# Scores of a pair of batches as one block of TensorE work, from a bank pool shared with the products, and the value products twelve places later

## Chip, cores, metric

The kernel runs on 1 core of one Trainium2 chip, in fp32. The metric is device time in microseconds (us). The result compares 4 runs of each kernel, made together; all are in the fast state. Times of one kernel agree within 0.2%, except where a range is given.

## The reference, cut to what matters

A batch is a graph of 128 nodes with 512 features; there are 128 batches, and every batch goes through four layers by itself. The fourth layer is attention with 8 heads, and the change is about its order.

```python
# x: (128, 128, 512); adj: (128, 128); all fp32
x = _layernorm(x + (adj @ x) @ w0 + bias0)            # layer 0
x = _layernorm(x + _L1_gnn_ref(x, W, a, beta, adj))   # layer 1: graph attention, one product with W
x = _layernorm(x + _L2_gnn_ref(x, adj, adj, b))       # layer 2: one product with adj, a maximum
# layer 3
q, k, v = (x @ w_qkv).reshape(b, n, 3, H, hd).transpose(2, 0, 3, 1, 4)   # H = 8, hd = 64
attn = softmax(where(adj == 0, -inf, q @ k.T * hd**-0.5))
o = (attn @ v) @ w_proj + b_proj
x = _layernorm(x + o + layernorm(o) * gamma + beta3)
```

## The kernel before

The kernel is written as chains, one or more per batch. A planner at build time asks every chain for its next step, takes the one that can start first (and of those the one with the lowest rank), and so fixes the order of instructions of each engine. On the chip the engines keep that order and wait for each other by semaphores. A step on TensorE names the buffers it needs; `tr`, `mm` and `sc` are PSUM tiles (`tr` and `mm` one bank each, `sc` two banks).

```python
BUFS = {
    "tr": 3, "mm": 3, "sc": 1,
    # ... buffers in SBUF: 16 batches (x) at once, 2 of xT, 6 of v, 2 of prT
}
TAIL = 8

def tiled(gr, before, bs=range(G)):          # G = 2: a pair of batches
    yield gr.qk
    if before:
        for b in range(G):
            yield before.rows[b]             # the pair before has its transposed probabilities
    got = yield use(
        "PE", 1.1 if len(bs) == 1 else 1.0,
        lambda: ("sc",) + ("pr",) * len(bs) + ("tr", "oT") * (G if before else 0),
        late=0.0, urgent=True,
    )
    gr.pr.extend(got[1 : 1 + len(bs)])
    score(gr, bs[0], got[0])                 # scores of the first batch
    if before:
        yield use("PE", 0.88 * G + 0.15, late=0.0, follow=True)
        attends(before, range(G), got[1 + len(bs) :])   # both attends of the pair before
    for b in bs[1:]:
        got = yield use("PE", 1.15, "sc", follow=True)  # waits for the one score buffer
        score(gr, b, got)                    # scores of the second batch

def score(gr, b, bs):
    sc = bank([P, 2, K, P], "sc")
    nodes = slice(b * P, (b + 1) * P)
    for c in range(K):
        for j in range(2):                   # 64 rows of the array: heads j = 0 and 1 beside each other
            rws = slice(j * HD, (j + 1) * HD)
            nc.tensor.matmul(sc[:, j, c, :], gr.qkT[rws, c, nodes], gr.qkT[rws, K + c, nodes],
                             start=True, stop=True)
    # ...

def attends(gr, bs, slots):
    for n, b in enumerate(bs):
        # ...
        p = bank([P, K, P], "tr")
        for c in range(K):
            for j in range(2):               # 64 columns of the array
                nc.tensor.matmul(p[j * HD : (j + 1) * HD, c, :],
                                 valued.v[:, (2 * c + j) * HD : (2 * c + j + 1) * HD],
                                 prT[:, j * K + c], start=True, stop=True)
        # ...

# in batch(i), after layer 2:
    plan.start(values(i, gr, valued), i + G)           # the product x @ w_v, with rank i + 2
    yield gr.scored[b]
    # ...
    nc.vector.tensor_tensor(pr, sc..., maskb..., op=ALU.add)   # one mask add of 128x1024
    give(bs)
```

Of the kernel before, what the change touches and what calls it, by code (L numbers as in the profile page):

```python
# [10 lines left out]
ALU = mybir.AluOpType  # L11
# [4 lines left out]
P = 128  # L16
D = 512
K = D // P
G = 2
H = 8  # L20
HD = D // H
# [5 lines left out]


BUFS = {
    "tr": 3, "mm": 3, "sc": 1,  # L30
    "x": 16, "yT": 4, "z": 2, "e": 2, "et": 1, "eT": 2, "ex": 2, "xT": 2, "v": 6, "qkT": 3,
    "pr": 2, "pt": 1, "xt": 2, "prT": 2, "oT": 2, "o": 2,
}
TAIL = 8
MARGIN = 1.0
LAND, ROW_LAND = 2.0, 0.0053

# [6 lines left out]
class Plan:  # L44
# [14 lines left out]
    def use(self, engine, work, take=None, late=0.05, urgent=False, follow=False):  # L59





        names = take if callable(take) else lambda: (take,) if take else ()
        return engine, work, names, late, 0 if follow else 1 if urgent else 2
# [4 lines left out]
    def done(self, event, late=0.0):  # L71
        event.left -= 1
        event.at = max(event.at, self.now + late)
        if not event.left:
            for r in event.chains:
                r["ready"] = max(r["ready"], event.at)
                self.step(r, None)

    def give(self, slot):
        name, i = slot  # L80
        self.slots[name][i] = self.now
# [13 lines left out]
    def at(self, r):  # L95
        engine, _, take, _, order = r["want"]
        early = min(MARGIN, r["ready"] / 20) if engine == "PE" and order else 0.0
        t = max(r["ready"] + early, self.free.get(engine, 0.0))
# [26 lines left out]
def gnn_stack_kernel(  # L125
# [17 lines left out]
    nc = tc.nc  # L143
# [9 lines left out]
    plan = Plan()  # L153
    use, give, done = plan.use, plan.give, plan.done

    def buf(shape, name):
        return work.tile(shape, F32, name=name, bufs=BUFS[name])

    def bank(shape, name):
        return ps.tile(shape, F32, name=name, bufs=BUFS[name])  # L160
# [40 lines left out]
    def product(lhs, rhs):  # L201

        p = bank([P, D], "mm")
        for k in range(K):
            nc.tensor.matmul(p, lhs(k), rhs(k), start=(k == 0), stop=(k == K - 1))  # L205
        return p
# [31 lines left out]
    maskb = const.tile([P, P], F32, name="maskb")  # L238
# [127 lines left out]
    class Group:  # L366


        def __init__(self):
            self.s = small.tile([P, G, 2], F32, name="s")  # L370
            self.logits = [Event(2) for _ in range(G // 2)]
            self.attention = [Event() for _ in range(G // 2)]
            self.turned, self.qk = Event(G), Event(K)
            self.rows, self.attended = ([Event() for _ in range(G)] for _ in range(2))
            self.scored = [Event() for _ in range(G)]
            self.heads, self.o, self.prT, self.sc, self.pr = {}, {}, [], {}, []
            self.eT, self.xT, self.qkT, self.slot, self.left = {}, None, None, {}, {}

        def read(self, name, of):
# [7 lines left out]
    def group(g):  # L387
        if g not in groups:
            groups[g] = Group()
            for h in range(G // 2):  # L390
                plan.start(attention1(groups[g], h), g * G + 2 * h - (8 if g * G >= NB - 8 else 0))
            for n in range(K):
                plan.start(query_key(groups[g], n // 2 * 2 + K * (n % 2)), g * G + n / K - (8 if g * G >= NB - 8 else 0))


            rank = g * G - (8 if g * G >= NB - 8 else 0)
            if g * G < NB - TAIL:
                plan.start(tiled(groups[g], groups.get(g - 1)), rank)
            else:
                for b in range(G):  # L400
                    plan.start(tiled(groups[g], None, (b,)), rank)
            if g * G >= NB - TAIL - G:
                for bs in ((0, 1),) if g * G < NB - G else ((0,), (1,)):
                    plan.start(attend(groups[g], bs), rank)
        return groups[g]
# [96 lines left out]
    def tiled(gr, before, bs=range(G)):  # L502
        yield gr.qk
        if before:
            for b in range(G):
                yield before.rows[b]
        got = yield use(
            "PE", 1.1 if len(bs) == 1 else 1.0,
            lambda: ("sc",) + ("pr",) * len(bs) + ("tr", "oT") * (G if before else 0),
            late=0.0, urgent=True,  # L510
        )
        gr.pr.extend(got[1 : 1 + len(bs)])
        score(gr, bs[0], got[0])
        if before:
            yield use("PE", 0.88 * G + 0.15, late=0.0, follow=True)
            attends(before, range(G), got[1 + len(bs) :])
        for b in bs[1:]:
            got = yield use("PE", 1.15, "sc", follow=True)
            score(gr, b, got)

    def score(gr, b, bs):

        sc = bank([P, 2, K, P], "sc")
        nodes = slice(b * P, (b + 1) * P)
        for c in range(K):
            for j in range(2):
                rws = slice(j * HD, (j + 1) * HD)
                nc.tensor.matmul(  # L528
                    sc[:, j, c, :], gr.qkT[rws, c, nodes], gr.qkT[rws, K + c, nodes],
                    start=True, stop=True,  # L530
                )
        gr.read("qkT", G)
        gr.sc[b] = sc, bs
        done(gr.scored[b], 0.15)

    def attend(gr, bs):
        for b in bs:
# [6 lines left out]
    def attends(gr, bs, slots):  # L544
        for n, b in enumerate(bs):
            valued, prT, bt = gr.heads.pop(b)

            p = bank([P, K, P], "tr")
            for c in range(K):
                for j in range(2):  # L550
                    nc.tensor.matmul(  # L551
                        p[j * HD : (j + 1) * HD, c, :],
                        valued.v[:, (2 * c + j) * HD : (2 * c + j + 1) * HD],
                        prT[:, j * K + c], start=True, stop=True,
                    )
            give(bt)
            give(valued.slot)
            gr.o[b] = p, slots[2 * n], slots[2 * n + 1]
        for b in bs:
            done(gr.attended[b], 0.2)  # L560

    def values(i, gr, event):
        b = i % G
        yield gr.turned
        bp = yield use("PE", 3.46, "mm", late=0.2)
        p = product(
            lambda k: gr.xT[:, k, b * P : (b + 1) * P], lambda k: wqkv_sb[:, k, 2 * D :]
        )
        bv = yield use("ACT", 0.6, "v", urgent=True)
        event.v = buf([P, D], "v")  # L570
        nc.scalar.copy(event.v, p)  # L571
        give(bp)
        gr.read("xT", G + K)
        event.slot = bv
        done(event)
# [19 lines left out]
    def batch(i):  # L595
        g, b = divmod(i, G)
        h = b // 2
        yield loaded[i]
        gr, xb = group(g), xs[i]
# [8 lines left out]
        p = product(lambda k: yT[:, k, :], lambda k: w0_sb[:, k, :])  # L608
# [8 lines left out]
        for j in range(2):  # L617
# [12 lines left out]
        p = product(lambda k: yT[:, k, :], lambda k: w1_sb[:, k, :])  # L630
# [15 lines left out]
        p = bank([P, D], "mm")  # L646
# [17 lines left out]
        biased = Event()  # L664
        plan.start(pool_add(xb, beta3_sb, biased), i)
        valued = Event()
        plan.start(values(i, gr, valued), i + G)

        yield gr.scored[b]
        sc, bs = gr.sc.pop(b)  # L670
        yield use("DVE", 1.22, urgent=True)
        pr, bpr = buf([P, H, P], "pr"), gr.pr.pop()
        nc.vector.tensor_tensor(  # L673
            pr, sc.rearrange("p j c m -> p (j c) m"),
            maskb[:, None, :].to_broadcast([P, H, P]), op=ALU.add,
        )
        give(bs)
        yield use("DVE", 1.22)
        nmx = small.tile([P, H], F32, name="nmx3")
        nc.vector.tensor_reduce(nmx, pr, axis=AX.X, op=ALU.max, negate=True)  # L680
# [21 lines left out]
        got = yield use("SP", 0.5, lambda: () if gr.prT else ("prT",) * G, late=4.0)  # L702
# [10 lines left out]
        p, ba, bo = gr.o.pop(b)  # L713
        yield use("ACT", 0.6, urgent=True)
        oT = buf([P, K, P], "oT")
# [4 lines left out]
        p = product(lambda k: oT[:, k, :], lambda k: wproj_sb[:, k, :])  # L720
# [22 lines left out]
    with tc.manual_schedule(  # L743
        engines={ENG.PE, ENG.DVE, ENG.Activation, ENG.Pool, ENG.SP}
    ):
        plan.start(loads(), 0)
        plan.start(adjacency(), 0)
        for i in range(NB):

            plan.start(batch(i), i if i < NB - 8 else i - 8)  # L750
        plan.run()
# [27 lines left out]
```

## Time and profile before

| | us |
|---|---|
| median time | 3294.3 (3293.8 to 3295.8) |
| span of the profiled run | 3291.2 |
| TensorE busy | 3269.0 |
| VectorE busy | 2663.6 |
| waits of TensorE that the profile lists | 9.7 |

The prediction below shows the lines on TensorE. How to read them: busy time of TensorE is no measure here, since the ends of matmuls are modelled; the distance from one start to the next is what a piece of work took. Two lines that come up again later are those of VectorE's mask add and of the division of probabilities by their sums (by-form groups of the kernel before; columns: line, engine, operation, tiles, shapes, count, then busy us and mean ns, then idle us before them and what ended it).

```profile
L691 DVE TENSOR_TENSOR pr<-pr,rs 128x1024 f32<-128x1024 f32 x128 | 192.0, 1500 | 4.4
L673 DVE TENSOR_TENSOR pr<-sc,maskb 128x1024 f32<-128x1024 f32 x128 | 156.2, 1220 | 57.3 <-PE sc L528 56.7
```

### The profile page before, as it was taken

The page shows a single profiled execution, that of the slowest core. Times are in us where ns is not written, and L with a number is a line of the kernel's source. Part 1 is how long each engine was busy: PE and PEld are TensorE (multiplying, and loading weights), DVE is VectorE, ACT ScalarE, POOL GpSimd, SP SyncE. Part 2 cuts the span into 40 slices and gives each one's busy share as a digit, 9 for nine tenths or more (in the row PEclk, how much of TensorE's full clock was granted, in tenths as well). Part 3 has the DMA queues.
Part 4 walks back from the last instruction along what each step waited for, and adds up shares of the span by engine and source line. Part 5 has one row for each costly group of instructions (what it writes and reads, how often), then busy time and mean ns, then how long its engine had stood idle before and what let it go on. Part 6 is the DMA issues. An engine that isn't in the chain of part 4 may idle for free.

```text
span 3291.2 us, 43479 instructions
## 1 busy us (share of the span) xinstructions
PE 3269.0 (99%) x14613; PEld 2064.7 (63%) x14613; DVE 2663.6 (81%) x5527; ACT 1186.9 (36%) x3457; POOL 965.6 (29%) x1031
## 2 busy tenths in 40 slices
PE   9999999999999999999999999999999999999998
PEld 5666666667565666566665656666566666656665
DVE  7879786996879868878788787869878787988867
ACT  3433433343433423333333333433333343334332
POOL 3223131331323314223233242313313131332322
PEclk9999999999999999999999999999999999999999
DMA  4323333223332333223233232332323323232232
GB/s 164 85 89 85 93 109 95 69 86 101 97 98 68 88 100 101 95 79 105 86 88 97 79 103 81 97 91 76 106 82 98 98 73 99 81 98 84 85 90 103
DMA packets 469760, 304.47 MB, mean 93 GB/s; under 512 B 319264, under 2 KB 401312, under 8 KB 469536
## 3 DMA queue, kind: packets, MB, share of 16 engines
q1 hardware_dynamic: 469536, 301.69, 30.8%
q8 instruction: 116, 1.90, 0.2%
q14 instruction: 108, 0.88, 0.1%
HBM read 158.93 MB, written 142.67 MB: 92 GB/s over the span
## 4 chain that ended last, share of the span: by engine, by line
PE 95%; DVE 3%; DMA 1%; SPq 1%; issue 0%; ACT 0%; POOL 0%; POOLq 0%; DVEq 0%; ACTq 0%
PE mm L205 51%; PE mm L485 27%; PE tr L213 6%; PE sc L528 4%; PE tr L551 3%; PE mm L647 3%; DVE st L171 0%; SPq L589 0%; DMA z<-s_d 0%; DVE x L640 0%; DVE x L192 0%; DVE x L612 0%; DMA s_d<-s 0%; DVE mv L173 0%; DVE pr L691 0%
## 5 line engine op out<-in xcount | busy, mean ns | idle before, releaser
L485 PE MATMUL mm<-xT,wqkv_sb 128*128 128x256 f32 x4096 | 908.4, 380 | 0.0
L205 PE MATMUL mm<-w_sb,yT 128*128 128x512 f32 x2048 | 904.6, 593 | 1.0 <-ACT yT L216 0.7
L178 POOL TENSOR_TENSOR rstd<-ve,neghalf 128x1 f32<-128x1 f32 x640 | 444.1, 694 | 1521.8 <-DVE ve L175 1267.0
L485 PEld LDWEIGHTS mm<-xT,wqkv_sb 128*128 128x128 f32 x4096 | 775.1, 190 | 146.8 <-issue 38.1
L205 PEld LDWEIGHTS mm<-w_sb,yT 128*128 128x128 f32 x2048 | 382.6, 190 | 452.5 <-issue 441.9
L205 PE MATMUL mm<-wproj_sb,oT 128*128 128x512 f32 x1024 | 453.6, 595 | 2.1 <-ACT oT L716 2.1
L205 PE MATMUL mm<-wqkv_sb,xT 128*128 128x512 f32 x1024 | 455.6, 593 | 0.0
L684 ACT ACTIVATE pr<-pr,nmx 128x128 f32<-128x128 f32 x1024 | 396.5, 389 | 109.1 <-DVE nmx L680 108.7
L171 DVE BATCH_NORM_STATS2 st<-x 128x6 f32<-128x512 f32 x512 | 349.4, 682 | 8.0 <-ACT x L655 5.4
L205 PEld LDWEIGHTS mm<-wproj_sb,oT 128*128 128x128 f32 x1024 | 192.1, 190 | 230.8 <-issue 220.5
L205 PEld LDWEIGHTS mm<-wqkv_sb,xT 128*128 128x128 f32 x1024 | 193.0, 190 | 216.4 <-issue 209.5
L198 POOL TENSOR_TENSOR x<-x,o 128x512 f32<-128x512 f32 x128 | 174.4, 1363 | 507.9 <-DVE o L724 507.5
L187 ACT ACTIVATE x<-x,nmr,rstd 128x512 f32<-128x512 f32 x256 | 205.1, 810 | 299.9 <-DVE nmr L185 286.3
L198 POOL TENSOR_TENSOR x<-x,beta_sb 128x512 f32<-128x512 f32 x128 | 174.4, 1365 | 208.0 <-DVE xt L661 185.6
L571 ACT COPY v<-mm 128x512 f32<-128x512 f32 x128 | 74.9, 586 | 427.1 <-PE mm L205 426.9
L216 ACT COPY yT<-tr 128x512 f32<-128x512 f32 x256 | 149.7, 585 | 210.5 <-PE tr L213 210.1
L619 DVE SCALAR_TENSOR_TENSOR scr<-x,wa_rows 128x512 f32<-128x512 f32 x256 | 200.2, 782 | 21.5 <-ACT x L187 16.4
L493 ACT ACTIVATE qkT<-mm 128x512 f32<-128x512 f32 x128 | 76.2, 595 | 363.4 <-PE mm L485 363.0
L198 POOL TENSOR_TENSOR x<-x,bias_sb 128x512 f32<-128x512 f32 x128 | 178.2, 1404 | 83.7 <-PE tr L213 74.3
L673 DVE TENSOR_TENSOR pr<-sc,maskb 128x1024 f32<-128x1024 f32 x128 | 156.2, 1220 | 57.3 <-PE sc L528 56.7
L691 DVE TENSOR_TENSOR pr<-pr,rs 128x1024 f32<-128x1024 f32 x128 | 192.0, 1500 | 4.4
L684 ACT ACTIVATION_READ_ACCUMULATOR pr<-pr,nmx 128x1 f32 x1024 | 192.4, 188 | 0.0
(64 smaller groups left out, 3501.2 us busy)
## 6 DMA issues: line engine op xcount, KB each, us to landing
p_d<-pt SPq DMA_DIRECT2D x128, 512.0 KB
prT<-p_d SPq DMA_DIRECT2D x128, 512.0 KB
x<-in_x SPq DMA_DIRECT2D x128, 256.0 KB
x_d<-xt SPq DMA_DIRECT2D x128, 256.0 KB
xT<-x_d SPq DMA_DIRECT2D x512, 64.0 KB
out<-x SPq DMA_DIRECT2D x128, 256.0 KB
z<-s_d SPq DMA_DIRECT2D x64, 128.0 KB
e_d<-et SPq DMA_DIRECT2D x64, 128.0 KB
```

What stands on the lines that cost most here:

```text
L171: nc.vector.bn_stats(st, src)
L178: nc.gpsimd.tensor_tensor(rstd, ve, neghalf, op=ALU.pow)
L187: nc.scalar.activation(xb, xb, AF.Identity, bias=nmr, scale=rstd)
L198: nc.gpsimd.tensor_tensor(dst, dst, other, op=ALU.add)
L205: nc.tensor.matmul(p, lhs(k), rhs(k), start=(k == 0), stop=(k == K - 1))
L213: nc.tensor.matmul(p[:, k, :], xb[:, k * P : (k + 1) * P], nodes, start=True, stop=True)
L216: nc.scalar.copy(yT, p)
L485: nc.tensor.matmul(p[:, j, :], wqkv_sb[:, k, (c + j) * P : (c + j + 1) * P], gr.xT[:, k, :], start=(k == 0), stop=(k == K - 1),)
L619: nc.vector.scalar_tensor_tensor(scr, xb, 1.0, wa_rows[:, j, :], op0=ALU.mult, op1=ALU.mult, accum_out=gr.s[:, b, j : j + 1],)
L673: nc.vector.tensor_tensor(pr, sc.rearrange("p j c m -> p (j c) m"), maskb[:, None, :].to_broadcast([P, H, P]), op=ALU.add,)
L684: nc.scalar.activation(pr[:, j, :], pr[:, j, :], AF.Exp, bias=nmx[:, j : j + 1], accum_out=sums[:, j : j + 1],)
L691: nc.vector.tensor_tensor(pr, pr, rs[:, :, None].to_broadcast([P, H, P]), op=ALU.mult)
```

## The change

The intent: put the scores of both batches of a pair side by side, followed by both attends of the preceding pair, so that TensorE enters its half-array modes once and leaves them once per pair. Two scores at once need four banks, so the score buffer is given up and products and scores share five banks. The mask add becomes two, one for each bank. The value products get rank i + 12 in place of i + 2; "twelve places later" and "late values" below mean this, counted from the batch's own rank.

```diff
-    "tr": 3, "mm": 3, "sc": 1,
+    "tr": 3, "mm": 5,
 TAIL = 8
+LATER = 12
@@ tiled
+        n = len(bs)
         got = yield use(
-            "PE", 1.1 if len(bs) == 1 else 1.0,
-            lambda: ("sc",) + ("pr",) * len(bs) + ("tr", "oT") * (G if before else 0),
+            "PE", 0.25 + 0.88 * n + (0.88 * G + 0.15 if before else 0),
+            lambda: ("mm", "mm", "pr") * n + ("tr", "oT") * (G if before else 0),
             late=0.0, urgent=True,
         )
-        gr.pr.extend(got[1 : 1 + len(bs)])
-        score(gr, bs[0], got[0])
+        for b in bs:
+            ps_b = [bank([P, K, P], "mm") for _ in range(2)]
+            # ... the same 8 matmuls, to ps_b[j][:, c, :]
         if before:
-            yield use("PE", 0.88 * G + 0.15, late=0.0, follow=True)
-            attends(before, range(G), got[1 + len(bs) :])
-        for b in bs[1:]:
-            got = yield use("PE", 1.15, "sc", follow=True)
-            score(gr, b, got)
+            attends(before, range(G), got)
+        # ... done(gr.scored[b]) for each
@@ batch
-        plan.start(values(i, gr, valued), i + G)
+        plan.start(values(i, gr, valued), i + LATER)
-        nc.vector.tensor_tensor(pr, sc..., maskb... [P, H, P], op=ALU.add)
-        give(bs)
+        for j in range(2):
+            # ... pr[:, j * K : (j + 1) * K] = sc[j] + maskb [P, K, P]
+            give(slots[j])
```

More of the change, by code (lines that the diff above doesn't have):

```diff
@@ L375, in __init__ @@
             self.scored = [Event() for _ in range(G)]
-            self.heads, self.o, self.prT, self.sc, self.pr = {}, {}, [], {}, []
+            self.heads, self.o, self.prT, self.sc = {}, {}, [], {}
             self.eT, self.xT, self.qkT, self.slot, self.left = {}, None, None, {}, {}
@@ L506, in tiled @@
                 yield before.rows[b]
+        n = len(bs)
         got = yield use(
-            "PE", 1.1 if len(bs) == 1 else 1.0,
-            lambda: ("sc",) + ("pr",) * len(bs) + ("tr", "oT") * (G if before else 0),
+            "PE", 0.25 + 0.88 * n + (0.88 * G + 0.15 if before else 0),
+            lambda: ("mm", "mm", "pr") * n + ("tr", "oT") * (G if before else 0),
             late=0.0, urgent=True,
         )
-        gr.pr.extend(got[1 : 1 + len(bs)])
-        score(gr, bs[0], got[0])
-        if before:
-            yield use("PE", 0.88 * G + 0.15, late=0.0, follow=True)
-            attends(before, range(G), got[1 + len(bs) :])
-        for b in bs[1:]:
-            got = yield use("PE", 1.15, "sc", follow=True)
-            score(gr, b, got)
-    def score(gr, b, bs):
-        sc = bank([P, 2, K, P], "sc")
-        nodes = slice(b * P, (b + 1) * P)
-        for c in range(K):
-            for j in range(2):
-                rws = slice(j * HD, (j + 1) * HD)
-                nc.tensor.matmul(
-                    sc[:, j, c, :], gr.qkT[rws, c, nodes], gr.qkT[rws, K + c, nodes],
-                    start=True, stop=True,
-                )
-        gr.read("qkT", G)
-        gr.sc[b] = sc, bs
-        done(gr.scored[b], 0.15)
+        for b in bs:
+            ps_b = [bank([P, K, P], "mm") for _ in range(2)]
+            nodes = slice(b * P, (b + 1) * P)
+            for c in range(K):
+                for j in range(2):
+                    rws = slice(j * HD, (j + 1) * HD)
+                    nc.tensor.matmul(
+                        ps_b[j][:, c, :], gr.qkT[rws, c, nodes], gr.qkT[rws, K + c, nodes],
+                        start=True, stop=True,
+                    )
+            gr.read("qkT", G)
+            gr.sc[b] = ps_b, got[:3]
+            got = got[3:]
+        if before:
+            attends(before, range(G), got)
+        for k, b in enumerate(bs):
+            done(gr.scored[b], 0.15 - 0.88 * (n - 1 - k) - (0.88 * G + 0.3 if before else 0.15))
     def attend(gr, bs):
@@ L666, in batch @@
         valued = Event()
-        plan.start(values(i, gr, valued), i + G)
+        plan.start(values(i, gr, valued), i + LATER)
         yield gr.scored[b]
-        sc, bs = gr.sc.pop(b)
-        yield use("DVE", 1.22, urgent=True)
-        pr, bpr = buf([P, H, P], "pr"), gr.pr.pop()
-        nc.vector.tensor_tensor(
-            pr, sc.rearrange("p j c m -> p (j c) m"),
-            maskb[:, None, :].to_broadcast([P, H, P]), op=ALU.add,
-        )
-        give(bs)
+        sc, slots = gr.sc.pop(b)
+        bpr = slots[2]
+        for j in range(2):
+            yield use("DVE", 0.69, urgent=True)
+            pr = pr if j else buf([P, H, P], "pr")
+            nc.vector.tensor_tensor(
+                pr[:, j * K : (j + 1) * K], sc[j], maskb[:, None, :].to_broadcast([P, K, P]),
+                op=ALU.add,
+            )
+            give(slots[j])
         yield use("DVE", 1.22)
```

## The prediction

> **What bounds the kernel now.** I read the page first for the busy shares, then the waits of TensorE, then TensorE's timeline, because the first two leave nothing but the third to save from. From the page, part 1, and the chain that ended last:
>
> ```profile
> span 3291.2 us, 43479 instructions
> ...
> PE 3269.0 (99%) x14613; PEld 2064.7 (63%) x14613; DVE 2663.6 (81%) x5527; ACT 1186.9 (36%) x3457; POOL 965.6 (29%) x1031
> ...
> PE 95%; DVE 3%; DMA 1%; SPq 1%; issue 0%; ACT 0%; POOL 0%; POOLq 0%; DVEq 0%; ACTq 0%
> ```
>
> TensorE (PE) is busy 99% of the span and is 95% of the chain. VectorE (DVE) is at 81%, so it has some 600 us of slack in total. The waits of TensorE, all the longest of them (columns: who waited on whom, total us, times, longest us):
>
> ```profile
> PE sc L528 <- DVE pr L673: 3.0, 3, 1.3
> PE mm L205 <- ACT oT L716: 2.1, 3, 0.7
> PE tr L213 <- DMA eT<-e_d: 1.5, 1, 1.5
> PE tr L321 <- POOL ident masks.py:199: 1.4, 1, 1.4
> ```
>
> The whole list adds up to 9.7 us, 0.3% of the span. So even a perfect schedule cannot win 1% by taking waits away. What is left is the time that TensorE spends while it is called busy: the page says that ends of matmuls are modelled, so I go by the distance from one start to the next instead. Two stretches of the timeline of TensorE, each around one pair's scores (L528, 64 rows of the array) and attends (L551, 64 columns of it); columns are start, length, engine, line:
>
> ```profile
> 1609.38 7.07 PE L485 MATMUL mm<-xT,wqkv_sb 128*128 128x256 f32 x32
> 1616.38 1.16 PE L528 MATMUL sc<-qkT 64*128 64x128 f32 x16
> 1617.47 1.97 PE L551 MATMUL tr<-prT,v 128*64 128x128 f32 x32
> 1619.37 1.16 PE L528 MATMUL sc<-qkT 64*128 64x128 f32 x16
> 1620.46 3.72 PE L485 MATMUL mm<-xT,wqkv_sb 128*128 128x256 f32 x16
> 1624.02 7.03 PE L205 MATMUL mm<-wproj_sb,oT 128*128 128x512 f32 x16
> ```
>
> ```profile
> 1653.26 3.60 PE L205 MATMUL mm<-w_sb,yT 128*128 128x512 f32 x8
> 1656.79 1.16 PE L528 MATMUL sc<-qkT 64*128 64x128 f32 x16
> 1657.88 1.97 PE L551 MATMUL tr<-prT,v 128*64 128x128 f32 x32
> 1659.77 1.13 PE L647 MATMUL mm<-x,adjT 128*128 128x512 f32 x2
> 1660.83 1.16 PE L528 MATMUL sc<-qkT 64*128 64x128 f32 x16
> 1661.92 7.13 PE L205 MATMUL mm<-wproj_sb,oT 128*128 128x512 f32 x16
> 1668.89 1.05 PE L213 MATMUL tr<-eT,x 128*128 128x128 f32 x8
> ```
>
> The reader is to see four things. (a) A product of 8 before a score takes 3.53 us from start to start (1653.26 to 1656.79), whereas a product of 16 amid others takes 6.87 (1624.02 to 1630.89, the next start), that is 3.43 per 8: **entering** a score costs about 0.09. (b) Products of 16 after a score take 6.97 (1661.92 to 1668.89), 0.10 over 6.87: **the first pair after leaving** costs 0.10. (c) The 2 matmuls of L647 squeezed between attends and a score take 1.06, against 0.86 for the same two elsewhere (1652.40 to 1653.26): both costs together, 0.20. (d) No wait stands beside any of these; the engine counts as busy throughout.
>
> **What the Trainium skill says.** "TensorEngine Tiling (Array Packing)", section Key Properties: changing the tiling mode, not just the tile, drains TensorE. The trace agrees: the single starts in it show 523 ns instead of 429 for the last matmul before a score, 201 to 203 ns for the last matmul of a score or attend block where neighbours are 105 apart, one start distance of 207 instead of 105 within each score block, and 533 instead of 429 for the first pair after. "Perfetto Trace Analysis", section Identifying the Most-Contended Engine, says that matmul busy share is a poor measure of headroom; it agrees in this sense, since the costs above lie inside the 99%. "PSUM — Partial Sum Buffer", section Specifications: eight banks of 2 KiB per partition. The kernel before uses 3 (tr) + 3 (mm) + 1 x 2 (sc) = 8, the one after 3 + 5 = 8, so nothing overflows.
>
> **The change part by part.**
>
> Part 1, the block. Before, one pair runs: score, both attends, (perhaps other work, because there is one score buffer and VectorE must empty it), score. After: score, score, both attends. The matmuls stay the same in number and shape. One score block of 16 instructions always takes 890 ns from its first start to its last, made up of 8 close pairs (7 ns apart), one distance of 207 and six of 105, plus 201 for the last: 1091. Two of them apart: 2 x 1091 = 2182 ns. Two joined: 16 close pairs 112, one 207, fourteen of 105 = 1470, last one 201: 1990. **Joined scores save 0.192 us per pair.** Where other work stood between attends and second score, its re-entry goes too: 0.104 for the first pair after attends and 0.094 for the entry, so **0.390 us per pair**.
>
> How many of each: of the 60 pairs made this way (the last 8 batches go singly and do not change), the trace has 31 with only the attends between the two scores, 26 with other work as well, and the first 3, at the start, with no attends but 16 instructions of L485 between. So 31 x 0.192 + 29 x 0.390 = 5.95 + 11.31 = 17.3 us, all of it on TensorE and so on the path that sets the end.
>
> Part 2, five banks instead of 3 + 2. The second score waited for VectorE to empty the single score buffer: 3.0 us in 3 waits, which go, since the second score has banks of its own. Sum with part 1: **20.3 us**. In exchange a block needs 4 of the 5 banks at once, so every product but the last one before the block must be emptied. A product takes 3.43 us on TensorE and its emptying on VectorE 0.69 (L612, L724), so the one before the last has usually been empty for 2 us. After the block, the next product takes the fifth bank, and the one after that the first score's bank, by which time the attends (1.90) and a product (3.43) have passed, while VectorE needs 4 x 0.69 = 2.8 us. I expect a few waits of up to a microsecond, not a regular one: 2 us in all, an estimate.
>
> Part 3, the mask add. One VectorE instruction of 128x1024 (L673, 128 times, 1220 ns) becomes two of 128x512 reading the product banks; the same kind and size is L724 at 684 ns. 2 x 684 - 1220 = 148 ns, times 128 = **19 us more of VectorE**, which goes from 81% to 82% and stays beside TensorE's work.
>
> Part 4, values rank twelve places later. The same 1024 value matmuls come in another place in TensorE's order, to be filled in where nothing older is ready. It costs nothing by itself. It can hold the transposed features (two buffers) longer; a pair comes every 3291/64 = 51 us, which is much room. It can shift the last 200 us, where 1.6 us of waiting stands now before the last two projections, by a few us either way.
>
> Sum: 3294.3 - 17.3 - 3.0 + 2 = **3276 us**, 0.56% less.
>
> **The rivals.** First, that the block of four banks takes away products' banks and TensorE waits on VectorE. For it: VectorE is at 81% and its order is fixed, so one late instruction delays the emptying; the score waits of today (up to 1.3 us) show that such delays occur. Against: those were on a buffer needed about 2 us later; here there are at least 2 to 3 us. If every third pair waited 1 us, it would give back 20 us: 3294, no change. Second, that VectorE becomes the bound through the extra 19 us and the four bunched urgent adds. Against: it would need 600 us more. It would only show as small waits, 3280 to 3285. Third, that joining buys more than the starts say: the looser order takes away the other waits in the middle (2.9 us) and at the end (2.4 us) as well. That gives 3269. Fourth, that holding values back starves the attends and so the end: the last 200 us grow by 10 us, 3286. I hold it for less likely, as idle TensorE takes the values whatever their rank.
>
> **Range and chances.** The saving of 17.3 us is counted and rests on constants that do not vary in the trace, so it is nearly certain; waits gained or lost make the rest. From 3268 (all rivals good) to 3288 (a third of pairs waiting a little). Faster by over 2% would need 66 us, and all the switching and waiting of TensorE that I can find is less than that: 0.01. Slower by over 2% would need a broken schedule: 0.01. Within 2%: 0.98.
>
> **What would show it.** In the profile after: on TensorE's timeline score groups of x32 from start to next start 1.99 us, followed by attends of 1.90, in 59 pairs, the first pair by scores alone; TensorE's busy time some 17 us less at equal instruction counts; no wait of a score for the mask add. Two mask adds per batch at about 0.69 us, VectorE busy about 19 us more. Wrong it would be if TensorE's waits grew beyond 10 us, above all products or scores waiting on the mask add or another emptying; if the second score began with another 207 ns (then the saving is 0.1 us per pair smaller, 6 us in all); or if the end after the last matmul (13 us now) grew.

## The result, and the profile after

The changed kernel took 3264.22 us (median of 4; 3264.02 to 3266.33) against 3294.29 us for the kernel before: 30.1 us less. The ratio is 0.9909, with a 95% interval from 0.9892 to 0.9927. A ratio here is the mean time of one kernel's fast runs over that of the other's fast runs of the same rounds, so it is not quite the ratio of the medians. The time lies under the range that I gave (3268 to 3288).

The page of the changed kernel, its span, its busy row and its chain by engine:

```profile
span 3262.3 us, 43708 instructions
...
PE 3247.4 (100%) x14613; PEld 2061.7 (63%) x14613; DVE 2643.7 (81%) x5655; ACT 1181.7 (36%) x3457; POOL 961.7 (29%) x1031
...
PE 100%; DVE 0%; issue 0%; POOLq 0%; ACT 0%; POOL 0%; DVEq 0%
```

TensorE runs the same 14613 matmuls in 21.6 us less busy time, and the chain is now TensorE alone. The waits of TensorE, all that the profile of the changed kernel lists:

```profile
PE tr L322 <- POOL ident masks.py:199: 1.4, 1, 1.4
PE mm L206 <- ACT yT L217: 0.7, 1, 0.7
PE tr L214 <- DVE adjT L329: 0.4, 1, 0.4
```

These three lie in the first 6 us. From there to the last matmul TensorE never waits for anything that the list shows. A block on the timeline of TensorE (start, length, engine, line; L521 is the scores, L549 the attends):

```profile
1507.35 3.60 PE L206 MATMUL mm<-w_sb,yT 128*128 128x512 f32 x8
1510.88 2.06 PE L521 MATMUL mm<-qkT 64*128 64x128 f32 x32
1512.86 1.97 PE L549 MATMUL tr<-prT,v 128*64 128x128 f32 x32
1514.76 2.05 PE L214 MATMUL tr<-adjT,x 128*128 128x128 f32 x16
1516.65 3.60 PE L206 MATMUL mm<-w_sb,yT 128*128 128x512 f32 x8
```

Both scores take 1.98 us from start to start (1510.88 to 1512.86), the attends 1.90 as before.

**Where the time went.** Every start of the trace was sorted by what stands before and after it. Each passage between ordinary matmuls (N), scores (S) and attends (A) has one cost, the same in every block: N to S 0.196 us, S to A 0.148, A to S 0.202, S to N 0.201, A to N 0.204, N to A 0.145. It is what the starts on either side are later than in a steady run. Multiplied by how often each occurs, and beside the start distances that are over 0.15 us too long ("waits", with those lengthened by a lowered clock):

| | before | after |
|---|---|---|
| passages NS, SA, AS, SN, AN, NA | 95, 59, 33, 69, 32, 6 | 64, 60, 1, 5, 63, 4 |
| their cost, us | 55.3 | 36.1 |
| waits, us | 10.6 | 2.0 |
| single distances 0.1 too long elsewhere | 23, so 2.3 us | 15, so 1.5 us |
| from the last matmul to the end, us | 13.0 | 12.9 |
| span, us | 3291.2 | 3262.3 |

The differences are 19.2 + 8.6 + 0.8 + 0.1 = 28.7 of the 28.9 us between the spans. What is left of a span without these rows is 3210.0 us before and 3209.8 after, so nothing else of size changed on TensorE. The forecast had 17.3 for the first, and 3.0 gained less 2 lost for the second. So switches came out close, and waits made the miss. VectorE went the other way from the forecast: here are the same two lines of it for the changed kernel.

```profile
L673 DVE TENSOR_TENSOR pr<-mm,maskb 128x512 f32<-128x512 f32 x256 | 162.5, 683 | 30.3 <-PE mm L521 30.2
L691 DVE TENSOR_TENSOR pr<-pr,rs 128x1024 f32<-128x1024 f32 x128 | 161.9, 1265 | 4.4
```

The 256 adds of 683 ns cover 162.5 us and not 175, as two neighbours overlap; that is 6.3 us more than before, not 19. The division, which nobody touched, took 30.1 us less.

### The profile page after: what moved, and what is told of

The parts are those of the page before. It is cut to its first block, busy times and chain, and to the rows that moved or that the text cites. A ratio compares the mean times of both kernels' runs of the same rounds, so it can differ in the third digit from the quotient of the medians.

```text
span 3262.3 us, 43708 instructions
## 1 busy us (share of the span) xinstructions
PE 3247.4 (100%) x14613; PEld 2061.7 (63%) x14613; DVE 2643.7 (81%) x5655; ACT 1181.7 (36%) x3457; POOL 961.7 (29%) x1031
## 4 chain that ended last, share of the span: by engine, by line
PE 100%; DVE 0%; issue 0%; POOLq 0%; ACT 0%; POOL 0%; DVEq 0%
PE mm L206 54%; PE mm L486 27%; PE tr L214 7%; PE mm L521 4%; PE tr L549 4%; PE mm L645 3%; PE tr L322 0%; DVE x L736 0%; DVE st L172 0%; DVE t L733 0%; DVE x L193 0%; PE tr L361 0%; DVE o L724 0%; ACT yT L217 0%; POOLq L775 0%
## 5 line engine op out<-in xcount | busy, mean ns | idle before, releaser
L486 PE MATMUL mm<-xT,wqkv_sb 128*128 128x256 f32 x4096 | 898.6, 379 | 0.0
L179 POOL TENSOR_TENSOR rstd<-ve,neghalf 128x1 f32<-128x1 f32 x640 | 456.8, 714 | 1421.1 <-DVE ve L176 1154.1
L199 POOL TENSOR_TENSOR x<-x,bias_sb 128x512 f32<-128x512 f32 x128 | 166.7, 1308 | 437.3 <-PE tr L214 428.1
L199 POOL TENSOR_TENSOR x<-x,beta_sb 128x512 f32<-128x512 f32 x128 | 166.2, 1301 | 217.4 <-DVE xt L659 214.9
L633 ACT ACTIVATE ex<-mm 128x512 f32<-128x512 f32 x128 | 76.2, 596 | 347.3 <-PE mm L206 346.6
L617 DVE SCALAR_TENSOR_TENSOR scr<-x,wa_rows 128x512 f32<-128x512 f32 x256 | 186.7, 729 | 15.6 <-ACT x L188 10.8
L673 DVE TENSOR_TENSOR pr<-mm,maskb 128x512 f32<-128x512 f32 x256 | 162.5, 683 | 30.3 <-PE mm L521 30.2
L691 DVE TENSOR_TENSOR pr<-pr,rs 128x1024 f32<-128x1024 f32 x128 | 161.9, 1265 | 4.4
```

The lines of the kernel that those rows point to most:

```text
L179: nc.gpsimd.tensor_tensor(rstd, ve, neghalf, op=ALU.pow)
L199: nc.gpsimd.tensor_tensor(dst, dst, other, op=ALU.add)
L486: nc.tensor.matmul(p[:, j, :], wqkv_sb[:, k, (c + j) * P : (c + j + 1) * P], gr.xT[:, k, :], start=(k == 0), stop=(k == K - 1),)
L617: nc.vector.scalar_tensor_tensor(scr, xb, 1.0, wa_rows[:, j, :], op0=ALU.mult, op1=ALU.mult, accum_out=gr.s[:, b, j : j + 1],)
L673: nc.vector.tensor_tensor(pr[:, j * K : (j + 1) * K], sc[j], maskb[:, None, :].to_broadcast([P, K, P]), op=ALU.add,)
L691: nc.vector.tensor_tensor(pr, pr, rs[:, :, None].to_broadcast([P, H, P]), op=ALU.mult)
```

## The experiments

Two questions: are passages between modes really what joined scores save, and what took away the waits? Twelve kernels ran; all gave correct results. The times of the kernel before in their jobs were 3292.2 to 3293.8, so times of different jobs compare to about 2 us.

**1. The attends back between the scores, nothing else.** The order of every other engine, and of all other matmuls, is identical to the changed kernel's.

```diff
-        for b in bs:
+        for m, b in enumerate(bs):
             # ... scores of b
-        if before:
-            attends(before, range(G), got)
+            if before and m == 0:
+                attends(before, range(G), got[3 * (n - 1) :])
```

> The changed kernel with one thing undone: in each of the 59 joined blocks the two attends stand between the two scores again (score, attends, score); the orders of all other engines and of all other matmuls are identical. Theory of switches: joined scores save 0.192 us per pair, so 59 x 0.192 = 11.3 us come back: 3264.2 + 11.3 = 3275.5, with waits of TensorE still under 3 us. Rival (the whole gain is waits that went, switches cost nothing): 3264, no change.

Measured: 3276.83 us (ratio to the kernel before 0.9951), 12.6 over the changed kernel; the spans differ by 12.6 too. The timeline of the same block in this run:

```profile
1516.09 1.16 PE L521 MATMUL mm<-qkT 64*128 64x128 f32 x16
1517.18 1.97 PE L549 MATMUL tr<-prT,v 128*64 128x128 f32 x32
1519.08 1.16 PE L521 MATMUL mm<-qkT 64*128 64x128 f32 x16
1520.17 2.05 PE L214 MATMUL tr<-adjT,x 128*128 128x128 f32 x16
```

From the first score to the next ordinary matmul it takes 4.08 us, in the changed kernel 3.88 (1510.88 to 1514.76): 0.20 per block, 59 times, 11.8 us. The profile lists no wait beside the same three at the start. Counted as in the table above, passages cost 47.8 us in this trace, 11.7 more than in the changed kernel. The rival, that switches cost nothing, is out.

**2. A larger dose: score, attend, score, attend.** Again all other orders are identical.

```diff
-        if before:
-            attends(before, range(G), got)
+            if before:                      # inside the loop over the two scores
+                attends(before, (m,), theirs[2 * m : 2 * m + 2])
```

> A dose of switches: the changed kernel with each joined block alternating (score, attend, score, attend); all other orders identical, as for the run with the attends in the middle, which measured 12.6 us over the changed kernel. Theory of switches, with constants read from the single starts: two score blocks apart cost 0.192 us, two attend blocks apart 0.162 us (16 instructions take 827 + 203 ns, twice, against 1695 + 203 for 32), so 59 x 0.354 = 20.9 us: 3285, waits of TensorE still under 3 us. Rival (what the middle run showed was a later start of the emptying, not switches): about 3277 again, or waits that grow.

Measured: 3285.54 us (ratio 0.9978), 21.3 over the changed kernel, where 20.9 was expected. The block in this run:

```profile
1520.48 1.16 PE L522 MATMUL mm<-qkT 64*128 64x128 f32 x16
1521.57 1.09 PE L549 MATMUL tr<-prT,v 128*64 128x128 f32 x16
1522.60 1.16 PE L522 MATMUL mm<-qkT 64*128 64x128 f32 x16
1523.69 1.09 PE L549 MATMUL tr<-prT,v 128*64 128x128 f32 x16
1524.71 2.05 PE L214 MATMUL tr<-adjT,x 128*128 128x128 f32 x16
```

It takes 4.23 us, 0.35 over the joined one. Passages cost 56.7 us in this trace, 20.6 more than in the changed kernel, and waits are 0.6 more: the time rises with the number of passages.

**3. Late values alone, in the kernel before.**

```diff
-        plan.start(values(i, gr, valued), i + G)
+        plan.start(values(i, gr, valued), i + 12)
```

> The kernel before with the one number changed: values twelve places later. If late values take the waits away: about 3286, waits of TensorE 2 to 3 us in place of 9.7. If not: 3294 with 8 to 12 us of waits. Switch counts may shift a little with the order; the timeline tells them.

Measured: 3283.91 us (ratio 0.9974, interval 0.9964 to 0.9985): 8.8 us less than the kernel before in its job. Passages cost 55.7 us, much as before; waits fell from 10.6 to 4.4, and the time after the last matmul from 13.0 to 10.1. (In the profile's own list, to which the expectation refers, waits fell from 9.7 to 4.5, less than the 2 to 3 expected.) All three waits of a score for the mask add are gone although the old single score buffer is still there. So the five banks are not needed to take these away.

From this run to the changed kernel the spans fall by 19.5 us (3281.8 to 3262.3): passages 55.7 to 36.1 are 19.6, waits give 2.4 more, and the stretch after the last matmul takes 2.8 back. In this order of adding the parts, late values make a third of the gain, and joining makes the rest.

**4. Joined scores with values at the old rank.**

```diff
-LATER = 12
+LATER = G
```

> The changed kernel with the values at their old rank, two places later in place of twelve. Switches stay joined. If the late values are what took away the 7 to 8 us of other waits that my prediction missed, they come back: about 3272, waits of TensorE 8 to 10 us. If the five shared banks or the joined block did it, nothing changes: 3264, waits near 2.5 us.

Measured: 3286.80 us (ratio 0.9982): 22.6 over the changed kernel, far more than the 8 that I expected, though passages cost 36.8, so the switches are still saved. The longest waits of TensorE:

```profile
PE tr L549 <- DMA prT<-p_d: 6.0, 2, 5.6
PE mm L206 <- ACT oT L716: 4.3, 4, 2.0
PE mm L486 <- DMA xT<-x_d: 4.0, 1, 4.0
PE mm L521 <- DVE x L610: 1.4, 1, 1.4
...
PE mm L521 <- DVE qkT L496: 0.7, 1, 0.7
```

Here too no score (L521) waits for the mask add (L673), so the five banks with the joining take these waits away as well. But two scores wait, 2.1 us together, until VectorE has emptied a bank of other work.

Counted by start distances, waits are 25.9 us. Only 4.7 of them lie in the middle of the run; 19.3 lie in the last 130 us. There a long wait costs twice: after the waits of 4.0 and 5.6 us the granted clock is 0.50 for a while.

**5. Late values only for the last 32 batches.**

```diff
-        plan.start(values(i, gr, valued), i + LATER)
+        plan.start(values(i, gr, valued), i + (LATER if i >= NB - 32 else G))
```

> The changed kernel, values late only for the last 32 batches, at the old rank for the 96 before. Theory of the end (late values are filler for the last 110 us, where the run with early values lost some 20 us): waits at the end go, those in the middle (3 to 4 us) stay: 3266 to 3270. Rival (late values matter all along, by keeping the whole order regular): 3280 or more.

Measured: 3269.05 us (ratio 0.9929). Waits: 2.9 us in the last 130 us, 2.0 in the middle. So late values for a quarter of the batches bring 17.8 of the 22.6 us, as the theory of the end expects; the rest is worth about 5.

**6. The values of the last 8 batches first.** The order of TensorE is the changed kernel's up to its last 6% (the first matmul that differs is number 13762 of 14613).

```diff
-        plan.start(values(i, gr, valued), i + LATER)
+        plan.start(values(i, gr, valued), i + (LATER if i < NB - 8 else -20))
```

> The changed kernel with the values of the last 8 batches put first in place of last; TensorE's order is identical up to the last 5%. Theory of the end (value products left over fill the last 30 us, in which the last attends wait for transposed probabilities): none is left there, a wait of 5 to 16 us on that transfer comes back with a halved TensorE clock after it, 3272 to 3285, while the middle stays free of waits. Rival (the end was lost in other runs for another reason, such as the order of the whole run): 3264 to 3267.

Measured: 3291.48 us (3290.36 to 3293.60; ratio 0.9996). The direction is as expected and the size is beyond it: 27.3 us, the whole gain of the change, lost by moving at most 8 of 128 value products. The end of this run:

```profile
3234.34 7.13 PE L206 MATMUL mm<-wproj_sb,oT 128*128 128x512 f32 x16
3250.14 1.97 PE L549 MATMUL tr<-prT,v 128*64 128x128 f32 x16 [8.67 <-DMA prT<-p_d]
3252.85 5.76 PE L206 MATMUL mm<-wproj_sb,oT 128*128 128x512 f32 x8 [0.73 <-ACT oT L716]
3271.17 1.98 PE L549 MATMUL tr<-prT,v 128*64 128x128 f32 x16 [12.56 <-DMA prT<-p_d]
3273.87 5.49 PE L206 MATMUL mm<-wproj_sb,oT 128*128 128x512 f32 x8 [0.73 <-ACT oT L716]
```

and the end of the changed kernel:

```profile
3221.53 7.03 PE L206 MATMUL mm<-wqkv_sb,xT 128*128 128x512 f32 x16
3228.49 1.97 PE L549 MATMUL tr<-prT,v 128*64 128x128 f32 x32
3230.39 3.70 PE L206 MATMUL mm<-wqkv_sb,xT 128*128 128x512 f32 x8
3233.93 7.03 PE L206 MATMUL mm<-wproj_sb,oT 128*128 128x512 f32 x16
3240.89 1.97 PE L549 MATMUL tr<-prT,v 128*64 128x128 f32 x32
```

The last attends (L549) need probabilities that go through ScalarE, VectorE and two transfers after the scores. In the changed kernel three value products (`wqkv_sb,xT`, x8 each) are left to fill that time. In the other nothing is left, so TensorE waits 8.67 and 12.56 us, and the projections that follow take 5.76 and 5.49 us in place of 3.70, at a lowered clock. "TensorE: Matmul & The Clock Gate", Part 1, says that the clock falls to half after some 3.4 us without work. These traces agree in part: in every run it was lowered in each wait of 4.0 us and more, and in experiment 4 it was not after one of 2.0 us. But it was often lowered sooner than the page says; the last section has the numbers.

**7 to 10. Other ranks, and other ends.** Values seven and twenty places later (`LATER = 7`, `LATER = 20`), a tail of four singly planned batches (`TAIL = 4`), and scores planned apart from the shared pool:

```diff
-            lambda: ("mm", "mm", "pr") * n + ("tr", "oT") * (G if before else 0),   # one step
+            lambda: ("mm", "mm") + ("pr",) * n + ("tr", "oT") * (G if before else 0),
+        # score; then a step for attends; then a step of its own, with ("mm", "mm"), for the other score
```

> Values seven places later: between the old two (3286.8) and twelve (3264.2) and twenty (3264.3). If the gain of late values is work held in reserve, it grows with the rank and levels off: 3265 to 3278. If each rank is luck, anything from 3264 to 3290.

> The changed kernel with values twenty places later in place of twelve. If twelve is simply enough to hold work in reserve: the same, 3262 to 3268, waits of 2 to 4 us. If every rank gives another order with its own luck, waits of 5 us or more, above 3268; if values come too late for the attends, long single waits on them.

> A try for a faster version: the changed kernel with 4 batches in the singly planned tail in place of 8; its order differs on TensorE in the last few blocks alone. If it joins the one pair of tail scores still apart: 0.2 to 0.4 us less than the changed kernel's 3264.2. If the attends of the end come later through it: 1 to 5 us more. No more than 5 us either way.

> Five banks shared by products and scores and values twelve places later, as in the changed kernel, but the scores of a pair planned apart as in the kernel before (score, attends, then the other score when its banks are free, other work in between where it is ready first). Theory of switches: between 11 us (nothing between) and 23 us (other work between in every pair) come back: 3276 to 3287, waits under 3 us. If the joined block is what took the other waits away, waits of 5 to 9 us come back as well: above 3285.

Measured: seven 3278.12 us (ratio 0.9953), twenty 3264.29 (0.9913), the short tail 3285.03 (0.9974), scores apart 3294.59 (1.0006). Seven lies at the upper edge of its range. My expectations for the last two missed: the short tail was thought to move at most 5 us and moved 21, and scores apart came out 8 us over the range of the switches. (It is "above 3285" too, but not for the reason given there: 20.4 of its 22.1 us of waits lie at the end, none in the middle.) Both have late values and both lost some 20 us at the end, most of it in one wait for the transfer of the probabilities (15.7 and 16.6 us). So rank 12 is not what counts. With the value products that start in the last 30 us before the last matmul, and the waits of the last 130 us, from the traces:

| run | value products in the last 30 us | waits in the last 130 us, us | median time, us |
|---|---|---|---|
| kernel before | 3 | 1.6 | 3294.3 |
| late values alone (3) | 3 | 1.6 | 3283.9 |
| changed kernel | 3 | 0 | 3264.2 |
| attends between (1) | 3 | 0 | 3276.8 |
| alternating (2) | 3 | 0 | 3285.5 |
| twenty later | 3 | 0 | 3264.3 |
| late for the last 32 (5) | 2 | 2.9 | 3269.1 |
| seven later | 0 | 13.3 | 3278.1 |
| values at old rank (4) | 0 | 19.3 | 3286.8 |
| scores apart | 0 | 20.4 | 3294.6 |
| tail of four | 0 | 20.5 | 3285.0 |
| last values first (6) | 0 | 27.5 | 3291.5 |

Every run with two or three left over loses under 3 us there, and every run with none loses 13 or more. The two runs that follow fit: three left and no wait, two left and 2.9 us. The kernel before had three left at rank i + 2; its order happened to leave them.

**11 and 12. The bank pool.** Four banks for scores alone, two for products, two for transposes and attends (`"tr": 2, "mm": 2, "sc": 4`); then six shared and two for transposes (`"tr": 2, "mm": 6`).

> Joined scores and late values, but the eight banks split anew: four for the scores alone, two for products, two for transposes and attends. It tells whether the shared pool matters, beside the joining. If products need more than two banks: many short waits of TensorE on the emptying by VectorE and ScalarE, 20 us or more: above 3284. If they do not: 3264.

> The eight banks as six for products and scores and two for transposes and attends, in place of five and three. Theory: after the changed kernel 2 us of waits are left, all in the first 6 us, so a sixth bank has nothing to win, while two transposes' banks can be short: the same, or up to 10 us slower: 3264 to 3274, with waits of transposes on ScalarE's copies if it is slower. The split with four score banks, two and two measured 3275.3.

Measured: 3275.34 us (3275.19 to 3278.66; ratio 0.9949) and 3269.50 (0.9927). The profiled run of the first is its slowest, at 3278.66. With banks of their own for the scores, the passages cost the same 36.1 us but waits are 12.0 us, 8.2 of them in the middle, where the profile lists products waiting for VectorE (1.9 us the longest, with a lowered clock after it): the loss is about 11 us, half of what I expected at least. The shared pool is worth that against this split. A sixth product bank taken from the transposes gains nothing and costs 5 us, within what was expected, though hardly by the wait that was named: transposes wait 0.5 us for ScalarE, while 2.9 us of waits stand in the last 130 us. In both runs with two banks for transposes, 50 start distances inside transposes are 47 ns longer, 2.3 us in all; the kernels before and after have none, and the cause is open. No run beat the changed kernel; the one with values twenty places later equals it.

## Why the prediction was wrong

- **What bounds the kernel** was right: TensorE, and there the starts and not the waits alone.
- **Part 1, joining**, was right in mechanism and nearly in size. Both scores were to take 1.99 us and take 1.98; experiments 1 and 2 gave 12.6 us for 11.3 and 21.3 for 20.9. The sum came out at 19.2, not 17.3. Its counts were misread: the trace has 33 pairs with only the attends between the scores, 26 with other work as well, and 5 with no attends between, of which just one is at the start. The other four (at 3020.0, 3117.8, 3224.0 and 3239.0 us) are the pairs of the last 8 batches. So 33 x 0.192 + 27 x 0.390 = 16.9 us were due. And the text said that the last 8 batches "go singly and do not change". In fact, three of their four pairs now stand side by side too (the trace has 63 joined blocks where 60 were made so), presumably because a single score needs only two of five banks, where one score buffer had kept them apart. At the 0.39 us of the prediction that is 1.2 us; attends of these batches that now stand beside other half-array work give 0.7, and the rounding of the constants 0.4.
- **Part 2** named the right 3.0 us, but the banks are not the only reason for them: these waits go with late values alone, with the old score buffer in place (experiment 3), and also with the banks and the joining alone (experiment 4). The 2 us of new waits, and the first rival, did not come with late values; without them 2.1 us of such waits did.
- **Part 3**, 19 us more of VectorE, was mis-sized: 6.3, since two adds overlap. VectorE as a whole fell by 19.9; the largest single drop is that of the division. Neither reached the time: TensorE waits for VectorE only once, 0.4 us at the start.
- **Part 4 is the step that failed**: "It costs nothing by itself", and then "a few us either way" at the end. I took the order in which a saturated engine does its work as free. Late values alone brought 8.8 us in the kernel before (experiment 3) and, given the joined block, 22.6 (experiment 4). Without them the change would have brought about 6 us and not 30. In the middle of the run, waits are 6.9 us before, 4.7 with the joining alone, 0.6 with late values alone and 0.3 with both. In the last 130 us they are 1.6, 19.3, 1.6 and 0. So of the 8.6 us of waits that went, 6.6 were in the middle and 1.6 at the end. The larger effect at the end does not show between these two kernels, because the kernel before had value products left there by the luck of its order. Near the end the value products are the only work that waits for nothing late, and whether some are left decides 13 to 27 us.
- **The sum**: 3276 forecast, 3264.2 measured. Waits account for 7.6 of the 11.8 us (8.6 gained in place of a net 1.0), passages for 1.9, single long distances for 0.8, and the medians differ by 1.1 us more than the profiled spans do.
- **The fourth rival** feared that late values starve the end. No run shows that: at twenty places the time is 3264.3. What starved the end was having no value products left, as at ranks 2 and 7 with joined blocks. The third rival had the right direction, waits going everywhere (3269), but blamed the joining. Its 2.9 and 2.4 us are also 1.1 too much: the list leaves 9.7 - 3.0 - 2.5 = 4.2 us without the waits of scores and those of the first 8 us.

What stays open is why late values also remove the waits in the middle (6.9 us before, 0.6 in experiment 3), which is about half of what the forecast missed. Each change of rank makes another order, and no run separates having work in hand from a lucky order there.

## What to carry to other kernels

On an engine that is busy all the time, count its mode passages by the distance between starts, and put work of one mode side by side: that saving could be worked out here, before the change was made, to some 2 us in 19. When a static order is changed, look at its last hundred microseconds first: keep back some work that depends on nothing late, to cover the latency of the last chain, because a long wait there (4 us and more in these runs) is paid again in a lowered clock. And judge two parts of a change together as well as apart: here the joined block without the late values would have looked hardly worth making.

## What the Trainium skill lacked or had wrong

- "TensorEngine Tiling (Array Packing)", Key Properties, says that changing the mode drains TensorE and gives no cost. For these fp32 blocks the runs show 0.20 us into row tiling, 0.20 out of either tiling, 0.15 from row to column tiling and 0.20 back; 59 extra round trips of the alternating kind cost 21.3 us.
- No page gives a figure for a block that follows another of the same mode with other banks: the second score block of a joined pair goes on at 105 ns, without the distance of 207 that begins every block standing alone.
- "SBUF — State Buffer", section Who interferes with whom, says that a VectorE instruction with two inputs in SBUF contends with a GpSimd instruction that reads SBUF. The traces agree and give a size, which the page lacks for this case: the division (L691, 128x1024) takes 1225 ns where no long GpSimd instruction runs, and 1683 on average in the 77 of 128 where one overlaps it for over 0.3 us in the kernel before. It depends mostly on which started first: 2028 on average in the 42 where the GpSimd instruction had, 1268 in the 35 where the division had. With the new order 61 are overlapped, 20 of them with GpSimd first, and they average 1308. That makes up the 30 us that the division takes less: 77 x 458 ns before, 61 x 83 ns after. The mask add, with one input in PSUM, hardly changes: 692 ns in the 8 of 256 that are overlapped so, 683 in the others.
- "TensorE: Matmul & The Clock Gate", Part 1, gives about 3.4 us without work as what halves the clock. Here less was enough. In experiments 4, 7 and 10 the granted clock fell to 0.50 between 2.0 and 2.6 us after a wait began, and still within 3.3 us counted from the start of the last matmul before it. In the profiled run of experiment 11 (four banks for scores) a wait of 1.93 us was enough: the granted clock in the stretch that began 2 us after it was 0.50, and 16 matmuls of a projection took 8.64 us from start to next start in place of 6.87. In experiment 4 a wait of 2.02 us was not. So a wait well under that figure can already be paid for twice; it is not shown which ones are.
